# Layer 3's half products grouped by four behind the scores, and the second layer's score matrices made in layer 1's tail

## The chip, the cores and the metric

The kernel runs on one core of a Trainium2 chip. The metric is the device time of one execution in microseconds (us). A core has five engines that run their own instruction streams and wait for each other through semaphores: TensorE (PE in the profile, its weight loads PEld), VectorE (DVE), ScalarE (ACT), GpSimd (POOL) and SyncE (SP), which here only starts transfers (DMAs). Matmuls write into PSUM, which has eight banks per partition; the other data lie in SBUF, 128 partitions wide.

## The reference, cut to what matters

The network has two layers. The first is a residual block of three "approximate matrix multiplications" with normalisations between them; the second is an attention layer and isn't touched. One such multiplication splits its input channels into groups (codebooks), scores each group against 16 centroids, takes a softmax over the 16 and multiplies the softmax by a table:

```python
scores = 2.0 * jnp.einsum('blcs,cks->blck', v, centroids) - jnp.sum(centroids * centroids, -1)[None, None]
attn = jax.nn.softmax(scores * inv_temp, axis=-1)
out = jnp.einsum('blck,cko->blo', attn, lut)
```

This is done three times: 1024 to 256 channels (here "layer 1"), 256 to 256 with 3x3 patches ("layer 2"), 256 to 1024 ("layer 3"), each followed by a batch norm over all images, so that a layer has to end before the next begins. There are 32 images of 14x14, in all 6272 tokens.

## The kernel before, in words

All matmuls are f32. Layers 1 and 2 work through 128 "units" each (`units`, lines 701 to 755): 16 pairs of images times 8 blocks of codebooks. A unit is: scores on TensorE (`score1` at line 879 with 32-row matmuls, `score2` at 999 with 64-row and at 1008 with 32-row ones), exponentials on ScalarE (566), a transpose on VectorE (578), sums, reciprocals and a second transpose on VectorE (597, 599, 605), the normalising product on GpSimd (612), a small repair of table rows by DMA (699), and the table product on TensorE (717, `lut`). The scores of a unit run three or four units ahead of its table product; `side(i)` and `side2(i)` hang other work into step i, and `at(i, piece)` puts a piece into layer 1's step i. Each engine executes what it is given in the order of the program.

A score matmul needs a matrix with the centroids laid out in blocks and a bias. `score_matrices` (341) and `centre` (331) build the matrices on VectorE from raw centroids and masks; `score_biases` (357) squares and centres the centroids on VectorE, and its inner function `biases` multiplies them out on TensorE (388, tile pb) and reduces the result on VectorE (392 to 398). For layer 2 this stands between the layers, at lines 959 to 987: the biases, the matrices w8, five products of an identity (`warm`, 561) and the matrices wm. Ahead of it there are the batch norm of layer 1 (310 to 327), the first padded images (`store_pair`, 909) written to DRAM as h1d, the patches read back from there (`load_patches`, 940), and the tables of layer 2 made ready (`less`, 674 and 675).

Layer 1 reads its pairs of images into three SBUF buffers in turn (pool p1x, `load_x`).

Layer 3 (lines 1066 to 1221) works through 14 chunks of 448 tokens. A chunk has 64 codebooks in 8 groups g of 128 rows; `rows[g]` holds the softmax and `luts[g]` the table. For each of the 8 output blocks m, `product` (1169) accumulates 7 whole products (groups 1 to 7, 128 rows, `whole`) and one half product: group 0 has only 64 rows, which are kept doubled (`double3`, 1116 and 1117) so that output m uses rows 0 to 63 and output m+1 rows 64 to 127, and the two run side by side. The order in a chunk is by pairs of outputs: whole products of m0, half products of m0 and m0+1, whole products of m0+1, then both are copied out (1200) with their statistics (1201). The scores of the next chunk (`score3`, 1093) come in two halves, b = 0 at the head of the chunk and b = 1 behind the first pair; their softmax follows behind outputs 1 and 3. The finished rows are spread by four DMAs and doubled by two (`spread3`, `double3`). A chunk's output is stored to DRAM (o3d, 1218). The first chunk differs: its first three outputs run group by group.

PSUM is divided into four banks for scores (ps_sc), three for outputs (ps_po) and one for small things (ps_tr, tag "tr"). At chunk 3 a transpose for the attention layer's tables (477, tile ph) uses ps_tr, and at chunk 13 the check for overflow does (622, pf).

A second copy of the three layers (`layers(True)`) is in the program for inputs whose exponentials overflow; it isn't executed here.

Of the kernel before, what the change touches and what calls it, by code (L numbers as in the profile page):

```python
# [10 lines left out]
F32 = mybir.dt.float32  # L11
AF = mybir.ActivationFunctionType
ALU = mybir.AluOpType
# [4 lines left out]
P = 128  # L18
# [132 lines left out]
def conv_preact_kernel(ctx: ExitStack, tc: tile.TileContext, a: dict, out: bass.AP):  # L151
# [176 lines left out]

    SHIFT = 32.0

    def centre(pool, i, name, v, k):

        rows, groups = v.shape[:2]
        mean = pool.tile([rows, groups], F32, tag=f"cmean{i}{name}", name=f"cmean{i}{name}")
        t = pool.tile([rows, 1], F32, tag=f"cinvt{i}{name}", name=f"cinvt{i}{name}")
        nc.vector.tensor_scalar(t, invs[i][:rows], k, None, ALU.mult)
        nc.vector.tensor_reduce(mean, v, AX.X, ALU.add)
        nc.vector.tensor_scalar(mean, mean, t, 1.0 / KC, ALU.mult, ALU.mult)
        nc.vector.scalar_tensor_tensor(v, v, t, bc(mean, 2, KC), ALU.mult, ALU.subtract)

    def score_matrices(pool, i, name, raw, mask):


        rows, groups = raw.shape[:2]
        w = pool.tile([rows, groups, P], F32, tag=f"cw{i}{name}", name=f"cw{i}{name}")
        centre(pool, i, name, raw, 2.0)
        for g in range(0, groups, 4):
            m = min(4, groups - g)
            nc.vector.tensor_tensor(
                w[:, g : g + m].rearrange("p g (c k) -> p g c k", k=KC),  # L350
                raw[:, g : g + m].unsqueeze(2).to_broadcast([rows, m, 8, KC]),
                mask.unsqueeze(1).unsqueeze(3).to_broadcast([rows, m, 8, KC]),
                ALU.mult,
            )
        return w

    def score_biases(ps_tr, pool, tmp, i, raw, rows, groups, mask, per, order=None):

# [8 lines left out]
        sq = room[:, : groups * KC].rearrange("p (g k) -> p g k", k=KC)  # L369
        spread = room[:, 512 : 512 + P]  # L370
        cols = sq
        bias = pool.tile([P, n], F32, tag=f"cbias{i}", name=f"cbias{i}")
        nc.vector.tensor_copy(spread.rearrange("p (c k) -> p c k", k=KC), bc(mask, 2, KC))

        nc.vector.tensor_tensor(sq, raw, raw, ALU.mult)
# [10 lines left out]
        def biases():  # L386
            pb = ps_tr.tile([P, 512], F32, tag="tr", name=f"pb{i}")[:, : n * KC]
            nc.tensor.matmul(
                pb, spread, cols.rearrange("p n k -> p (n k)"), start=True, stop=True
            )  # L390
            pv = pb.rearrange("p (n k) -> p n k", k=KC)
            nc.vector.tensor_tensor(pv, pv, bc(kmask, 1, n), ALU.mult)
            b = pool.tile([P, n], F32, tag=f"cb{i}", name=f"cb{i}")
            nc.vector.tensor_reduce(b, pv, AX.X, ALU.add)
            dst, src = bias, b
            if order is not None:
                dst, src = order(bias), order(b, True)
            nc.vector.tensor_scalar(dst, src, -SHIFT, None, ALU.add)
# [92 lines left out]
    def layers(exact, early=None):  # L491
# [142 lines left out]
        two = ExitStack()  # L634
        tsp = two.enter_context(tc.tile_pool(name="p12t", bufs=1))

        def unit_tiles(n):

            ts = []
            for k in range(n):  # L640
                t = tsp.tile([P, 4, NCP], F32, tag=f"t{k}", name=f"t{k}")
                nc.gpsimd.memset(t[:, :, N2:], 1.0)
                ts.append(t)
            return ts
# [114 lines left out]
        stats1 = big.tile([P, 2, NP, 6], F32, tag="stats", name="stats1")  # L759
        with ExitStack() as s:  # L760
            once = s.enter_context(tc.tile_pool(name="p1c", bufs=1))
            xp = s.enter_context(tc.tile_pool(name="p1x", bufs=3))
            sm = s.enter_context(tc.tile_pool(name="p1s", bufs=2))
            st = s.enter_context(tc.tile_pool(name="p1tt", bufs=1 if exact else 2))

# [8 lines left out]

            def load(p):
                def piece():
                    xts[p] = load_x(xp, p)
                    v = slice(2 * p, 2 * p + 2)
                    for k, f in enumerate(
                        gn_pieces(sm, ps_tr, xts[p], gn_a[:, :, v], gn_b[:, :, v])  # L780
                    ):
                        at(first(p) + k, f)

                return piece
# [52 lines left out]
            xts[0] = load_x(xp, 0)  # L837
            for b in range(2):
                luts[b][1]()
            xts[1] = load_x(xp, 1)  # L840
            for b in range(2, 8):
                luts[b][1]()
            if not exact:
# [29 lines left out]
            def score1(u):  # L873
                p, b = divmod(u, 8)
                scs = []
                for j in range(4):
# [2 lines left out]
                    nc.tensor.matmul(sc, w1[r, b, :], xts[p][r, b, :], start=True, stop=True)  # L879
                    scs.append(sc)  # L880
                return scs

            units(
                AHEAD,
# [14 lines left out]
        with ExitStack() as s:  # L899
# [56 lines left out]
            luts2[3][2]()  # L956
            for b in range(4):
                luts2[b][4]()
            bias2, biases = score_biases(
                ps_tr,  # L960
                once,
                st,
                2,
                raw[2],
                72,
                32,
                mask2,
                1,
                lambda t, src=False: t.rearrange("p (h j b) -> p h b j", h=2, j=4)
                if src  # L970
                else t.rearrange("p (h b j) -> p h b j", h=2, b=4),
            )
            w8 = score_matrices(once, 2, "8", raw8, mask64)
            biases()
            warm(5, pads[0][:, :N2])

            centre(once, 2, "1", raw1, 2.0)
            wm = once.tile([P, 2, 4, P], F32, tag="wm", name="wm")
            for h in range(2):
                nc.vector.tensor_tensor(  # L980
                    wm[:, h].rearrange("p b (c k) -> p b c k", k=KC),
                    raw1[:, h].unsqueeze(1).unsqueeze(2).to_broadcast([P, 4, 8, KC]),
                    mask32.rearrange("p (b c) -> p b c", c=8)
                    .unsqueeze(3)
                    .to_broadcast([P, 4, 8, KC]),
                    ALU.mult,
                )

            def score2(u):
                p, b = divmod(u, 8)  # L990
# [75 lines left out]
        with ExitStack() as s:  # L1066
# [76 lines left out]
                less3(7, h, by_act)  # L1143
            relu3(1, 0)
            relu3(1, 1)
            nxt = [score3(1, 0)]
            rows = sum(map(split3, t3), [])
            softmax(st, 0, t3[0], *token_major(st, t3[0]), steps=(1, 1, 2))
            spread3(rows, (1,))
# [3 lines left out]
            softmax(st, 1, t3[1], *token_major(st, t3[1]), steps=(1, 1, 2))  # L1153
            spread3(rows, range(4, 8))
            double3(rows[0])
            for k in range(NCH):
                more = k + 1 < NCH
                if more and k:
                    nxt = [score3(k + 1, 0)]
                elif not more and not exact:  # L1160
                    add_up(2, 2 * NCH)
                    again = overflow(once)
                if early and k > 0:
# [4 lines left out]
                def product(m, g, r=slice(0, P), start=False, stop=False):  # L1168
# [5 lines left out]
                        stop=stop,  # L1174
                    )

                def whole(m):
                    for g in range(1, CT):
                        product(m, g, start=m % 2 == 0 and g == 1, stop=m % 2 == 1 and g == 7)

                for m0 in range(0, CT, 2):
                    for m in range(m0, m0 + 2 + (k + m0 == 0)):
                        if m not in pos:
                            pos[m] = ps_po.tile([P, 512], F32, tag="po", name="po3")[:, :NC]

                    if k + m0 == 0:
                        for g in range(1, CT):
                            for m in range(3):
                                product(m, g, start=g == 1)
                    elif k > 0 or m0 != 2:  # L1190
                        whole(m0)
                    for m in (m0, m0 + 1):
                        r = slice(64 * (m - m0), 64 * (m - m0) + 64)
                        product(
                            m, 0, r, start=m > m0 and k + m0 > 0, stop=m == m0 or k + m0 == 0
                        )
                    if k + m0 > 0:
                        whole(m0 + 1)
                    for m in (m0, m0 + 1):
                        nc.scalar.copy(o[:, m, :], pos[m])  # L1200
                        nc.vector.bn_stats(stats3[:, m, k, :], o[:, m, :])  # L1201
                        if not more:
                            bn_sum(mv3[:, m, :], stats3, m)
                        if more and m == 0:
                            nxt.append(score3(k + 1, 1))
                        if m in (4, 5):
                            relu3(k + 2, m - 4)
                        if more and m in (1, 3):
                            t = nxt[m // 2]
                            softmax(st, 2 * k + 2 + m // 2, t, *token_major(st, t))  # L1210
                            if m == 1:
                                then = split3(t)
                                spread3(then, (1, 2, 3))
                            else:
                                then += split3(t)
                                spread3(then, range(4, 8))
                                double3(then[0])
                nc.sync.dma_start(o3d[:, :, k * NC : (k + 1) * NC], o)
                if more:
                    rows = then  # L1220
            bn_final(once, None, 3, range(CT), sc3, bi3, mv3)
        act.close()
        return again
# [802 lines left out]
```

## Time and profile before

| What | Value |
|---|---|
| time, median of 3 runs (lowest, highest) | 3702.62 us (3702.26, 3704.74) |
| time of the profiled execution | 3700.99 us |
| span of the profiled execution | 3699.2 us |
| mean granted clock of TensorE | 0.994 |
| layer 1's last table product to layer 2's first scores | 836.7 to 856.3 us |
| layer 2's first table product | 880.1 us |
| layer 3's products, first and last | 1860.3 to 2549.5 us |
| stores of layer 3, o3d | 14 of 1792 KB |

Times in the profile count from the span's start. A row of a timeline gives the start, the duration, engine, line, operation, the tiles written and read, the form (partitions x elements) and how many instructions it merges; in brackets stands the idle time of the engine before it and what ended that. A matmul row's duration contains its way through the array, so neighbours overlap; the distance from start to start tells the pace.

### The profile page before, as it was taken

The numbers are of one execution on the slowest core, as the hardware profiler recorded it, in microseconds if no ns is written. First come the engines' busy times: TensorE is split into PE (matmuls) and PEld (weight loads), VectorE is DVE, ScalarE is ACT, GpSimd is POOL, SyncE is SP. The second block draws the span as 40 slices with busy tenths as digits, with TensorE's granted clock in tenths as the row PEclk, the third lists the DMA queues.
The fourth block names the chain that finished last, engine by engine and source line by source line (L and its number), as shares of the span: only waits on it lengthen the run. The fifth ranks groups of instructions, "written<-read, shape, count | busy, mean of one in ns | idle before, by whom it ended". The sixth has DMA issues, their size and how long they took to land. (4 is left out here: it accounts for less than half of the span.)

```text
span 3699.2 us, 49702 instructions
## 1 busy us (share of the span) xinstructions
PE 3626.1 (98%) x16229; PEld 1999.0 (54%) x16229; DVE 2979.5 (81%) x4291; ACT 1717.9 (46%) x3895; POOL 2307.5 (62%) x1398
## 2 busy tenths in 40 slices
PE   8999999999999999999999999998999999999999
PEld 4555555554554445445444444444666666666666
DVE  8999999987888888888753334333799999999996
ACT  5555555543333333333322222213776676676675
POOL 6999999993454445445421111111988888888887
PEclk9999999999999999999999999999999999999999
DMA  3111111115444434444221111103123233233321
GB/s 110 43 46 44 43 37 32 43 33 134 89 92 87 94 75 94 85 95 84 72 51 53 45 45 45 38 33 130 44 79 93 82 87 91 86 84 85 90 75 44
DMA packets 238331, 260.14 MB, mean 70 GB/s; under 512 B 33380, under 2 KB 235692, under 8 KB 238064
## 3 DMA queue, kind: packets, MB, share of 16 engines
q1 hardware_dynamic: 237280, 256.51, 26.2%
q8 instruction: 131, 2.15, 0.3%
q14 instruction: 136, 1.11, 0.1%
q10 hardware_dynamic: 784, 0.37, 0.0%
HBM read 164.04 MB, written 77.09 MB: 65 GB/s over the span
## 5 line engine op out<-in xcount | busy, mean ns | idle before, releaser
L612 POOL TENSOR_TENSOR t<-t,r 128x1664 f32<-128x1664 f32 (+3 forms) x288 | 1008.5, 3502 | 952.0 <-DVE r L605 771.7
L717 PE MATMUL po<-t,lut 128*128 128x392 f32 x3840 | 1332.1, 499 | 2.7 <-DMA t<-spare 2.5
L717 PEld LDWEIGHTS po<-t,lut 128*128 128x128 f32 x3840 | 710.5, 190 | 593.3 <-issue 122.0
L566 ACT ACTIVATE t<-sc,cbias 128x392 f32<-128x392 f32 (+1 forms) x1136 | 580.0, 594 | 946.2 <-issue 476.1
L1536 PE MATMUL mm<-y,lut 128*128 128x392 f32 x2048 | 710.4, 493 | 0.1
L1169 PE MATMUL po<-t,lut 128*128 128x448 f32 (+1 forms) x1792 | 662.1, 551 | 1.6 <-issue 1.6
L578 DVE STREAM_TRANSPOSE tt<-t 128x1664 f32<-128x1664 f32 (+1 forms) x284 | 541.8, 1908 | 105.4 <-ACT t L566 99.7
L605 DVE STREAM_TRANSPOSE r<-rc 128x1664 f32<-128x1664 f32 (+1 forms) x284 | 546.5, 1924 | 20.8 <-DVE rc L599 0.5
L1758 DVE SCALAR_TENSOR_TENSOR pa<-y,lepe_w,pa 128x406 f32<-128x406 f32 x900 | 537.4, 637 | 3.8 <-PE pa L1740 0.3
L1536 PEld LDWEIGHTS mm<-y,lut 128*128 128x128 f32 x2048 | 370.4, 188 | 243.1 <-issue 6.1
L1169 PEld LDWEIGHTS po<-t,lut 128*128 128x128 f32 (+1 forms) x1792 | 308.7, 189 | 352.0 <-issue 351.3
L597 DVE TENSOR_REDUCE sm<-tt 128x104 f32<-128x832 f32 (+2 forms) x284 | 423.2, 1490 | 7.6 <-POOL tt L581 2.0
L1201 DVE BATCH_NORM_STATS2 stats<-o 128x6 f32<-128x448 f32 x112 | 68.9, 617 | 432.0 <-ACT o L1200 432.0
L581 POOL TENSOR_TENSOR tt<-tt 128x832 f32<-128x832 f32 x128 | 248.4, 1941 | 9.3 <-DVE tt L578 9.3
L599 DVE RECIPROCAL rc<-sm 128x104 f32<-128x104 f32 (+1 forms) x284 | 229.4, 808 | 9.8
L1200 ACT COPY o<-po 128x448 f32<-128x448 f32 x112 | 59.2, 530 | 326.4 <-PE po L1169 278.5
L999 PE MATMUL sc<-patch,cw 64*128 64x392 f32 x1024 | 204.0, 514 | 1.4 <-ACT lut L675 1.4
L614 ACT ACTIVATE sm<-sm 128x104 f32<-128x104 f32 (+1 forms) x284 | 84.9, 299 | 215.3 <-DVE rc L599 213.6
L999 PEld LDWEIGHTS sc<-patch,cw 64*128 64x128 f32 x1024 | 87.5, 184 | 109.5 <-issue 62.0
L1721 POOL TENSOR_TENSOR qr<-qr,zb 128x784 f32<-128x784 f32 x64 | 117.8, 1852 | 42.7 <-DMA zb<-zd 35.1
L1389 ACT ACTIVATE w<-x,tb,gn_a 128x196 f32<-128x196 f32 x248 | 128.3, 517 | 33.4 <-DVE x L1403 19.9
L1545 ACT ACTIVATE e<-mm,kbd 128x392 f32<-128x392 f32 x128 | 74.6, 583 | 145.2 <-PE mm L1536 143.7
(191 smaller groups left out, 4103.7 us busy)
## 6 DMA issues: line engine op xcount, KB each, us to landing
patch<-h1d SPq DMA_DIRECT2D x248, 162.8 KB
x<-in_x_dram SPq DMA_DIRECT2D x32, 784.0 KB
o3d<-o SPq DMA_DIRECT2D x14, 1792.0 KB
x<-in_x_dram SPq DMA_DIRECT2D x64, 392.0 KB
out_dram<-x SPq DMA_DIRECT2D x64, 392.0 KB
o<-o3d SPq DMA_DIRECT2D x62, 392.0 KB
h1d<-pad SPq DMA_DIRECT2D x96, 225.0 KB
t<-spare SPq DMA_DIRECT2D x960, 12.2 KB
```

The lines of the kernel that those rows point to most:

```text
L566: nc.scalar.activation(t[:, j, : sc.shape[1]], sc, AF.Identity if exact else AF.Exp, bias=bias[:, j : j + 1],)
L578: nc.vector.transpose(tt, tf)
L581: nc.gpsimd.tensor_tensor(tv[:, :, :8], tv[:, :, :8], tv[:, :, 8:], ALU.add)
L597: nc.vector.tensor_reduce(sm, tv, AX.X, ALU.add)
L599: nc.vector.reciprocal(rc, sm)
L605: nc.vector.transpose(r, bc(rc, 2, KC))
L612: nc.gpsimd.tensor_tensor(tf[:, v], tf[:, v], r[:, v], ALU.mult)
L717: nc.tensor.matmul(po[h], luts[b][:, j, h * P : (h + 1) * P], ts[u % len(ts)][:, j, :N2], start=(b == 0 and j == j0), stop=(b == 7 and j = ...
L999: nc.tensor.matmul(sc, w8[r, 8 * h + 4 * (j // 2) + g], grid(pbuf[n % NPB][r, j // 2, g]), start=True, stop=False,)
L1169: nc.tensor.matmul(pos[m], luts[g][r, m * P : (m + 1) * P], rows[g][r], start=start, stop=stop,)
L1536: nc.tensor.matmul(pv(), w[kt][:, m0 : m0 + P], ywin(p, first + kt), start=(kt == 0), stop=(kt == 3),)
L1758: nc.vector.scalar_tensor_tensor(acc, neighbours(p, c, offset(k)), lw[:, c, k : k + 1], acc, ALU.mult, ALU.add,)
```

## The change

Layer 3: the scores' second half moves from the first to the second half of the chunk, and both halves stand behind the whole products of output 0 or 4. Right behind them run the half products of four outputs, so four accumulators are open: three in ps_po and every fourth output in ps_tr. Then output m0 is copied out, the softmax of the scores follows, and the whole products of the other three outputs run, each with its own copy-out. In the first chunk the fourth output's whole products run ahead of the half products.

Layer 2's matrices: `matrices2` is hung into layer 1's step 125, the bias product into step 127 (there are 128 steps). Its results lie in one SBUF buffer on the other side of the memory, which until then was the third buffer for images; its temporaries lie in a buffer of layer 1. The code between the layers and the five warming products go.

```diff
-            xp = s.enter_context(tc.tile_pool(name="p1x", bufs=3))
+            xp = s.enter_context(tc.tile_pool(name="p1x", bufs=2))
...
-                    xts[p] = load_x(xp, p)
+                    xts[p] = load_x(kept if p % 3 == 1 else xp, p)
...
+            def matrices2():
+                room = kept.tile([P, CT, N2], F32, tag="x", name="room2")
...
+                bias2, biases = score_biases(
...
+                parts[2] = score_matrices(cut, 2, "8", raw8, mask64, w8), wm, bias2
+
+
+                centre(cut, 2, "1", raw1, 2.0)
+                for h in range(2):
+                    nc.vector.tensor_tensor(
+                        wm[:, h].rearrange("p b (c k) -> p b c k", k=KC),
...
+                at(8 * NP - 1, biases)
+
+            at(8 * NP - 3, matrices2)
...
-            bias2, biases = score_biases(
...
-            w8 = score_matrices(once, 2, "8", raw8, mask64)
-            biases()
-            warm(5, pads[0][:, :N2])
-
-            centre(once, 2, "1", raw1, 2.0)
...
+            w8, wm, bias2 = parts[2]
...
-                if more and k:
-                    nxt = [score3(k + 1, 0)]
-                elif not more and not exact:
+                if not more and not exact:
...
                 def whole(m):
                     for g in range(1, CT):
-                        product(m, g, start=m % 2 == 0 and g == 1, stop=m % 2 == 1 and g == 7)
+                        product(m, g, start=m % 4 == 0 and g == 1, stop=m % 4 > 0 and g == 7)
...
+                def halves(m0):
+                    for m in (m0, m0 + 1):
                         if m not in pos:
+                            pool, tag = (ps_tr, "tr") if m % 4 == 3 else (ps_po, "po")
+                            pos[m] = pool.tile([P, 512], F32, tag=tag, name="po3")[:, :NC]
+                        r = slice(64 * (m - m0), 64 * (m - m0) + 64)
+                        first = k + m0 // 4 == 0
+                        product(m, 0, r, start=m % 4 > 0 and not first, stop=m % 4 == 0 or first)
+
+                def out(m):
+                    nc.scalar.copy(o[:, m, :], pos[m])
+                    nc.vector.bn_stats(stats3[:, m, k, :], o[:, m, :])
...
+                def then(b, t):
+
+                    softmax(st, 2 * k + 2 + b, t, *token_major(st, t))
+                    rows3[k + 1] = rows3.get(k + 1, []) + split3(t)
+                    spread3(rows3[k + 1], range(4 * b + (b == 0), 4 * b + 4))
+                    if b:
+                        double3(rows3[k + 1][0])
...
+                for m0 in (0, 4):
+                    pos[m0] = ps_po.tile([P, 512], F32, tag="po", name="po3")[:, :NC]
+                    if k + m0 == 0:
...
+                    else:
                         whole(m0)
...
+                    t = None
+                    if more and (k or m0):
+                        t = score3(k + 1, m0 // 4)
+                    elif more:
+                        t = nxt
+                    halves(m0)
+                    halves(m0 + 2)
+                    out(m0)
+                    if t is not None:
+                        then(m0 // 4, t)
+                    for m in range(m0 + 1, m0 + 4):
+                        if k + m0 > 0:
+                            whole(m)
+                        out(m)
```

## The prediction

> **What bounds the kernel now.** I read the page first, then TensorE's and its weight loads' timeline in layer 3 and layer 2, then every engine's timeline between layers 1 and 2, last the rows in which VectorE waits beside GpSimd. The page's groups:
>
> ```profile
> PE 3626.1 (98%) x16229; PEld 1999.0 (54%) x16229; DVE 2979.5 (81%) x4291; ACT 1717.9 (46%) x3895; POOL 2307.5 (62%) x1398
> L1169 PE MATMUL po<-t,lut 128*128 128x448 f32 (+1 forms) x1792 | 662.1, 551 | 1.6 <-issue 1.6
> ```
>
> TensorE is busy in 98% of the span and idles 1.6 us in all ahead of layer 3's products, which are 662 us of the time. Whatever shortens TensorE's stream there comes off the end; other engines only matter if they become late. TensorE's timeline gives a chunk's length:
>
> ```profile
> 1907.96 1.03 PE L1093 MATMUL sc<-out,cw 32*128 32x448 f32 x8
> ...
> 1956.98 1.03 PE L1093 MATMUL sc<-out,cw 32*128 32x448 f32 x8
> ```
>
> From one chunk's first scores to the next chunk's: 49.02 us, without a stall. Each f32 product is two instructions ("steps"). The weight loads show the step:
>
> ```profile
> 2098.02 0.19 PEld L1169 LDWEIGHTS po<-t,lut 128*128 128x128 f32 x1 [0.19 <-issue]
> 2098.39 0.19 PEld L1169 LDWEIGHTS po<-t,lut 128*128 128x128 f32 x1 [0.19 <-issue]
> 2099.24 0.30 PEld L1169 LDWEIGHTS po<-t,lut 64*128 64x128 f32 x4 [0.65 <-issue]
> 2100.19 0.30 PEld L1169 LDWEIGHTS po<-t,lut 128*128 128x128 f32 x2 [0.65 <-issue]
> 2100.67 0.19 PEld L1169 LDWEIGHTS po<-t,lut 128*128 128x128 f32 x1 [0.19 <-issue]
> ```
>
> Whole products load every 0.375 us, and a load sits one step ahead of its matmul: the load of 2098.39 belongs to the matmul of 2098.77. From there to 2100.67 there are four steps, two of them a pair of half products (64x128; both halves run in one step). They take 1.90 us, not 4 x 0.375 = 1.50. The two changes of shape, into the pair and out of it, cost 0.40 us, 0.20 each. The period says the same: 112 whole steps, 4 x 2 of half pairs and 2 x 2 of scores are 124 x 0.375 = 46.50 us; 2.52 us are left for 12 changes of shape, 0.21 each. I take 0.205.
>
> **Layer 3, the main term.** Now each chunk has six short groups (four half pairs, two of scores), each fenced by whole products: 12 changes. After the change each half of a chunk runs whole, scores, two half pairs, whole: 3 changes, 6 a chunk. No step is added or dropped. Is one pair behind another free, and scores behind halves not? Layer 2 has both kinds of neighbour:
>
> ```profile
> 1404.37 0.96 PEld L999 LDWEIGHTS sc<-patch,cw 64*128 64x128 f32 x8 [0.56 <-ACT pad L909]
> 1405.89 0.31 PEld L1008 LDWEIGHTS sc<-pad,wm 32*128 32x128 f32 x8 [0.56 <-issue]
> 1406.76 0.30 PEld L717 LDWEIGHTS po<-t,lut 128*128 128x128 f32 x2 [0.56 <-issue]
> ```
>
> Four steps of 64-row pairs take 1.52 us, two of 32 rows 0.87; a step is 0.33 us there, so each group is its steps and 0.20 (half a change at either end): pairs behind each other cost nothing extra, going from 64 to 32 rows a full change. The other direction, 32 to 64, is in no row. Bounds: 0 and 0.205 us; nearest is the row just read, so 0.205. "TensorEngine Tiling (Array Packing)", Key Properties, in the Trainium skill says that every change of the tiling mode drains TensorE, which speaks against a free step from scores to halves; by it the term stays as I have it, without it it would be 25 x 0.205 = 5.1 us better.
>
> Count: chunks 1 to 12 lose 6 changes each, 72; chunk 0 (its first scores are made ahead) goes from 8 to 5; chunk 13, without scores, from 8 to 4. 79 x 0.205 = **16.2 us off**.
>
> What must still hide: the second scores move from about 12 to 29 us into the chunk. Their chain to finished rows, from before:
>
> ```profile
> 2069.47 1.03 PE L1093 MATMUL sc<-out,cw 32*128 32x448 f32 x8
> ```
>
> ```profile
> 2081.04 3.99 POOL L612 TENSOR_TENSOR t<-t,r 128x1792 f32<-128x1792 f32 x1 [35.31 <-DVE r L605]
> ```
>
> ```profile
> 2094.78 2.44 SPq L1113 DMA_DIRECT2D t<-t  x4
> 2097.26 0.51 SPq L1116 DMA_DIRECT2D t<-t  x1
> 2098.90 0.51 SPq L1117 DMA_DIRECT2D t<-t  x1
> ```
>
> Scores to the end of GpSimd's product: 2069.47 to 2085.03, 15.6 us (exponentials, one copy-out, VectorE's four passes, the product). The copies that spread and double the rows begin 0.03 us behind the second tile's product and their last packets end by 2101.0, 6.3 us. Together 21.9. New chunk: 46.5 + 6 x 0.205 = 47.7 us; the second scores start at 23.9 + 5.25 + 0.2 = 29.3, so the doubled rows[0] lie ready at 51.2. The next chunk's halves want them at 47.7 + 5.25 + 0.2 + 0.95 = 54.1: 2.9 us to spare. Spread rows 4 (ready 46.3) are wanted at 50.1. On SP's queue the 1.8 MB store of o3d is issued behind these copies, as now. The fourth accumulator: output 3's bank is copied 0.6 us after 23.9 and wanted again past 30; ScalarE's copy of output 1 waits in its queue behind the sum of the softmax until about 16.5, its bank is wanted at 30. VectorE and GpSimd do the same work, idle for most of layer 3. All hidden.
>
> One price: at chunk 3 the attention tables put one transpose on TensorE that waits for VectorE. Now the scores (1 us) run during that wait (TensorE idles 1.48 us ahead of L477); after the change they stand behind it: **+1.0 us**. By "TensorE: Matmul & The Clock Gate", Part 1, an idle window of about 3.4 us halves the clock; the wait grows to 2.5, so by the page nothing more comes; if it did, the row for it is chunk 13's overflow wait, behind which a run of 14 steps takes 7.1 us in place of 5.46, so +1.7 as my bound.
>
> **Second layer's matrices.** Between the layers:
>
> ```profile
> 848.31 2.07 PE L674 MATMUL less<-lut,less_last 128*128 128x512 f32 x2 [5.46 <-ACT lut L675]
> 850.17 1.91 PE L388 MATMUL pb<-croom 72*128 72x512 f32 x2
> 851.88 4.53 PE L561 MATMUL sc<-pad,ident 128*128 128x392 f32 x10
> 856.34 1.59 PE L999 MATMUL sc<-patch,cw 64*128 64x392 f32 x8
> ```
>
> The bias product (1.7) and ten warming matmuls (4.5) leave this place: 6.2 us is the most that the first scores can gain. What they wait on now is VectorE's masks (wm ends at 855.8). That work, 9.9 us (840.25 to 846.41, 853.68 to 855.80, 852.12 to 853.77), goes into a hole in layer 1's tail:
>
> ```profile
> 834.77 0.57 DVE L754 BATCH_NORM_STATS2 stats<-out 128x6 f32<-128x392 f32 x1 [11.28 <-ACT out L727]
> ```
>
> 11.28 us from 823.49. But GpSimd's last normalising product runs in it, 823.62 to 827.33, and two rows show VectorE standing still for such a product:
>
> ```profile
> 1333.52 3.39 DVE L338 TENSOR_SCALAR cmean3b<-cmean3b,cinvt3b 128x2 f32<-128x2 f32 x1
> 2624.11 1.19 DVE L1668 TENSOR_TENSOR kmm<-ks,hmean 128x32 f32<-128x32 f32 x1
> ```
>
> The first usually takes 0.23, the second 0.18; each ended 0.05 us behind a GpSimd product. The moved work has both forms at its head, so it starts at 827.3 and ends at 837.2. The bias product adds 2 x 0.43 = 0.86 us to TensorE ahead of the last unit, so layer 1's last statistics are wanted at 835.6 and come at 837.2: everything up to the patches shifts by 2.5 us. Then: last table product 850.8, scores 852.7, at half clock (0.85 us for a 0.43 step, as in the rows at 850) until 856.3, done 857.0, exponentials 859.1 instead of 860.84: 1.7 gained. The second scores wait for patches, issued until 855.54 now, 858.0 then, landing some 3 us later, and give back 0.3. From there VectorE's 6.5 us per unit, without a gap from 860.87 to 887, carries the lead into layer 2: **1.5 us off**. Bounds: 5.3 off (no wait at GpSimd, full clock, 6.2 - 0.86); 3 worse (patches and half clock without the warm-up eat all). The middle lies nearest to the rows. x's third buffer on the other side is the same rotation: nothing.
>
> **Sum**, against the profiled execution (3700.99; span 3699.2, 1.8 around it): -16.2 + 1.0 - 1.5 = -16.7, 3684.3. The runs' median, 3702.62, lies 1.63 higher: I predict **3686** (3702.62 - 16.7 = 3685.9). A difference under 0.2% (7.4 us) can't be told from none.
>
> **Rivals.** *Scores to halves is free*: 5.1 better, 3681. For: no row has this direction; against: the opposite one costs 0.20. 8%. *The price belongs to each short group, whatever its neighbours*: layer 3 gives nothing, 3702. For: every short group in layer 3 today stands alone; against: layer 2's four steps in a row. 6%. *Rows come late, slower*: the doubled rows[0] become the wait in place of the changes of shape. The place is the halves of each next chunk, it decides from 2.9 us of delay; 4.2 us eat the gain (1.3 us x 13), and a double held behind the 1.8 MB store (8.5 us from 2107.5) would stall 13 x 5.6 = 73 us: 3759. Against: the order on SP's queue, and no chunk stalls in the trace. 4%. The forecast's own case has 80%; 2% is left for mishaps.
>
> **Chances.** Faster by over 0.2%: forecast and first rival, 0.88; within: the second and part of the rest, 0.07; slower 0.05. Range: the forecast's ends are 3686 - 3.8 - 1 and + 4.5 + 1.7 + 0.6 (second term's bounds, clock, 0.20 or 0.21 a change), the first rival's end lies inside: 3680 to 3693.
>
> **What would show it.** Chunk period 47.7 us; four half pairs as loads x8 in one group behind the scores; no idle time ahead of L1169; the moved masks starting at 827, VectorE's first statistics near 837; first scores near 852. Wrong if loads between scores and halves keep 0.375, if TensorE waits for the doubled rows, or if layer 2's first products don't come before 880.

## The result, and the profile after

The changed kernel takes 3693.75 us (median of 13 runs, 3689.95 to 3698.86), the kernel before 3700.96 us (13 runs, 3697.59 to 3704.74). The ratio is 0.998, with a 95% interval of 0.9973 to 0.9988: 7.2 us faster, where 16.7 were forecast. The profiled execution of after took 3698.86 us (span 3696.9), the slowest of its 13 runs, that of before 3700.99.

Layer 3 got shorter at about the forecast pace. From the page of after, the busy time of the engines and layer 3's products (before: 662.1 us):

```profile
PE 3613.6 (98%) x16219; PEld 2004.2 (54%) x16219; DVE 2984.0 (81%) x4291; ACT 1723.5 (47%) x3895; POOL 2307.0 (62%) x1398
...
L1196 PE MATMUL po<-t,lut 128*128 128x448 f32 (+1 forms) x1792 | 649.8, 547 | 1.3 <-DMA t<-t 1.3
```

TensorE's timeline of after, from one pair of scores to the next (start, duration, what; lines stand 44 further down than before in the attention layer, 27 or 28 in layer 3):

```profile
1937.23 1.03 PE L1121 MATMUL sc<-out,cw 32*128 32x448 f32 x8
1938.19 23.02 PE L1196 MATMUL po<-t,lut 64*128 64x448 f32 x64
1961.14 1.03 PE L1121 MATMUL sc<-out,cw 32*128 32x448 f32 x8
```

Half a chunk takes 23.91 us, so a chunk 47.82 where 49.02 were before and 47.7 forecast. The weight loads show the order: scores, the eight instructions of four half products in one run, whole products:

```profile
1936.39 0.19 PEld L1196 LDWEIGHTS po<-t,lut 128*128 128x128 f32 x1 [0.19 <-issue]
1937.23 0.31 PEld L1121 LDWEIGHTS sc<-out,cw 32*128 32x128 f32 x8 [0.65 <-issue]
1938.19 0.30 PEld L1196 LDWEIGHTS po<-t,lut 64*128 64x128 f32 x4 [0.65 <-issue]
1938.68 0.19 PEld L1196 LDWEIGHTS po<-t,lut 64*128 64x128 f32 x2 [0.18 <-issue]
1939.05 0.19 PEld L1196 LDWEIGHTS po<-t,lut 64*128 64x128 f32 x2 [0.18 <-issue]
1939.90 0.30 PEld L1196 LDWEIGHTS po<-t,lut 128*128 128x128 f32 x2 [0.65 <-issue]
```

Scores to halves: 0.96 us for two steps of 0.375, a full change of 0.21. Half a chunk is 62 steps, 23.25 us; 0.66 are left for three changes, 0.22 each. Counted over the whole of layer 3, the rows that the loads use change 161 times in the trace of before and 82 times in that of after: 79 fewer, as forecast.

From its first to its last product, layer 3 takes 677.6 us in place of 689.2, so 11.6 of the forecast 15.2 appear there (the rest is in the point on chunk 3). But only 2.3 us of them reach the end of the span. What gives them back is the attention layer, of which the change touches no line. Counted from its first matmul to the end it took 1139.6 us before and takes 1148.3 after. The row of its costliest VectorE group, first from the page of before, then from that of after:

```profile
L1758 DVE SCALAR_TENSOR_TENSOR pa<-y,lepe_w,pa 128x406 f32<-128x406 f32 x900 | 537.4, 637 | 3.8 <-PE pa L1740 0.3
```

```profile
L1802 DVE SCALAR_TENSOR_TENSOR pa<-y,lepe_w,pa 128x406 f32<-128x406 f32 x900 | 540.4, 636 | 19.5 <-PE pa L1784 17.1
```

The same 900 instructions of the same length, but VectorE now waits 17.1 us for TensorE's products ahead of them. VectorE, GpSimd, TensorE and ScalarE execute the attention layer in another order in the two traces; whether that explains the wait, the first experiment tells.

That order isn't written down in the kernel. The layer's pieces are collected in a `Plan`, whose `write` plays through a list of estimated costs and lets each free engine take its next ready piece. It walks the engines like this:

```python
engines = {p[0] for p in self.pieces}
...
            for e in engines:
```

`engines` is a set of strings such as "PE" and "DVE". The order of a set of strings differs from one process to the next, and VectorE and GpSimd compete in this list for a lock that one of them holds at a time (`locked`, `port`). Played through for all 120 orders of the five, the list gives two schedules only: with GpSimd ahead of VectorE 1163.8 us long by its own estimates, with VectorE ahead 1171.6. GpSimd's instructions of the attention layer stand in before's trace as the first schedule has them, in after's as the second has them; the traces of the next section say the same of all of VectorE's and ScalarE's too (before's order is that of before with GpSimd first, after's that of after with VectorE first, instruction by instruction). So each build of either kernel draws one of two programs, and the two that were compared had drawn differently.

### The profile page after: what moved, and what is told of

Same layout as the page of the kernel before. It is cut to its first block, busy times and chain, and to the rows that moved or that the text cites. A ratio compares the mean times of both kernels' runs of the same rounds, so it can differ in the third digit from the quotient of the medians.

```text
span 3696.9 us, 49649 instructions
## 1 busy us (share of the span) xinstructions
PE 3613.6 (98%) x16219; PEld 2004.2 (54%) x16219; DVE 2984.0 (81%) x4291; ACT 1723.5 (47%) x3895; POOL 2307.0 (62%) x1398
## 5 line engine op out<-in xcount | busy, mean ns | idle before, releaser
L1196 PE MATMUL po<-t,lut 128*128 128x448 f32 (+1 forms) x1792 | 649.8, 547 | 1.3 <-DMA t<-t 1.3
L1802 DVE SCALAR_TENSOR_TENSOR pa<-y,lepe_w,pa 128x406 f32<-128x406 f32 x900 | 540.4, 636 | 19.5 <-PE pa L1784 17.1
L579 ACT ACTIVATE t<-sc,room 128x392 f32<-128x392 f32 x512 | 258.6, 587 | 600.5 <-issue 374.3
L579 ACT ACTIVATE t<-sc,cbias 128x392 f32<-128x392 f32 (+1 forms) x624 | 320.5, 597 | 418.9 <-PE sc L894 154.8
L1196 PEld LDWEIGHTS po<-t,lut 128*128 128x128 f32 (+1 forms) x1792 | 316.6, 190 | 331.3 <-issue 329.8
L1027 PE MATMUL sc<-patch,room 64*128 64x392 f32 x1024 | 207.7, 517 | 2.7 <-DMA patch<-h1d 2.7
L1027 PEld LDWEIGHTS sc<-patch,room 64*128 64x128 f32 x1024 | 88.9, 186 | 114.2 <-issue 67.6
L1546 ACT ACTIVATE y<-x,gb,ga 128x196 f32<-128x196 f32 x256 | 122.5, 541 | 46.6 <-POOL gb L1509 46.6
```

What stands on the lines that cost most here:

```text
L579: nc.scalar.activation(t[:, j, : sc.shape[1]], sc, AF.Identity if exact else AF.Exp, bias=bias[:, j : j + 1],)
L1027: nc.tensor.matmul(sc, w8[r, 8 * h + 4 * (j // 2) + g], grid(pbuf[n % NPB][r, j // 2, g]), start=True, stop=False,)
L1196: nc.tensor.matmul(pos[m], luts[g][r, m * P : (m + 1) * P], rows[g][r], start=start, stop=stop,)
L1802: nc.vector.scalar_tensor_tensor(acc, neighbours(p, c, offset(k)), lw[:, c, k : k + 1], acc, ALU.mult, ALU.add,)
```

## The experiments

**Theory:** the change is worth about what was forecast, and the draw of the attention layer's order takes about 8.5 us of it. **Rival:** the change itself slows the attention layer, say by leaving queues or buffers in another state.

### Both kernels with both orders

One line, in each kernel; the second order has "DVE" and "POOL" exchanged:

```diff
-        engines = {p[0] for p in self.pieces}
+        engines = ["POOL", "PE", "DVE", "ACT", "SP"]
```

(In these expectations the attention parts of 1139.6 and 1148 us are counted from that layer's first matmul, not from layer 3's last product as they say.)

> The kernel before, with one line fixed: the recording layer of the attention layer walks its five engines in a set of strings, whose order is drawn anew in each build; here the list is fixed with GpSimd ahead of VectorE. Of the 120 possible orders the layer's own planner makes only two schedules, 1163.8 us long by its own estimates with GpSimd first and 1171.6 with VectorE first, and the profiled program of before has the first of them, that of after the second. Theory A (the two profiles differ behind layer 3 by the draw, not by the change): as the profile of before, about 3701 us, attention part 1139.6 us from the last product of layer 3 to the end of the span. Theory B (the change slows the attention layer): also about 3701.

> The kernel before with the list fixed the other way, VectorE ahead of GpSimd. Theory A: the attention part grows by 8 to 9 us (7.8 by the planner's estimates, 8.8 between the two profiles), so about 3709.5 us. Theory B (the order is worth nothing, the change itself slows the attention layer): about 3701, as with GpSimd first.

> The changed kernel with GpSimd ahead of VectorE. Theory A: the change's own gain appears, 3693.75 less 8 to 9 us, so about 3685.5 us and a ratio to the first kernel of this set of about 0.996. Theory B: about 3693.8 us, with an attention part of 1148 us.

> The changed kernel with VectorE ahead of GpSimd, the order that the profiled program of after has. Theory A: as measured for the change, about 3694 us, attention part 1148 us. Theory B: about 3694 us too; the set tells the theories apart by the other two kernels.

Measured, with the profiled execution's parts (us):

| | median (runs) | lowest, highest | layer 3, first to last product | attention, first matmul to end |
|---|---|---|---|---|
| before, GpSimd first | 3701.42 (11) | 3697.90, 3703.60 | 689.2 | 1140.1 |
| before, VectorE first | 3709.85 (11) | 3707.67, 3714.33 | 689.2 | 1148.1 |
| after, GpSimd first | 3682.99 (5) | 3682.60, 3685.65 | 675.7 | 1139.0 |
| after, VectorE first | 3692.02 (5) | 3688.06, 3694.75 | 673.0 | 1147.4 |

The attention part follows the order alone, 8.0 and 8.4 us, with either kernel; so does VectorE's wait (in the two kernels of before, 0.3 us with GpSimd first and 16.9 with VectorE first, put down to the same products). From the page of after with GpSimd first, then with VectorE first (the shares of the chain of work that ended last, and the group from above):

```profile
PE 16%; DVE 6%; ACT 6%; POOL 2%; issue 1%; DMA 0%; DVEq 0%; SPq 0%; ACTq 0%; POOLq 0%
...
L1802 DVE SCALAR_TENSOR_TENSOR pa<-y,lepe_w,pa 128x406 f32<-128x406 f32 x900 | 538.8, 640 | 3.6 <-PE pa L1784 0.3
```

```profile
PE 12%; DVE 10%; ACT 4%; POOL 2%; issue 2%; DMA 2%; SPq 0%; DVEq 0%; POOLq 0%; ACTq 0%
...
L1802 DVE SCALAR_TENSOR_TENSOR pa<-y,lepe_w,pa 128x406 f32<-128x406 f32 x900 | 542.1, 640 | 19.3 <-PE pa L1784 17.0
```

The rival falls. With the order held, the change is worth 18.4 us (GpSimd first) and 17.8 (VectorE first), the difference of the medians of five and eleven runs. The kernel before that was run beside this set took 3708.41 us, which fits VectorE first, 3709.85: it seems to have drawn the other order this time. Against it the four ratios are 0.9979 (0.997 to 0.9988), 1.0005 (0.9996 to 1.0014), 0.9932 (0.9919 to 0.9946) and 0.9959 (0.9945 to 0.9972).

### Each part alone, and the price of a change of shape

The parts are the diff of the change cut in two: layer 3's lines, and all the others. In the third kernel the scores are moved away from the halves:

```diff
+                    t = None
+                    if more and (k or m0):
+                        t = score3(k + 1, m0 // 4)
+                    elif more:
+                        t = nxt
...
                         whole(m0)
-                    t = None
-                    if more and (k or m0):
-                        t = score3(k + 1, m0 // 4)
...
                     halves(m0)
```

> Layer 3's new order alone, with layer 2's matrices made where they were before, and the engine list fixed with GpSimd first. The prediction's steps: -16.2 for 79 changes of shape and +1.0 for the wait of the table transpose, so 3701.4 - 15.2 = 3686.2 us. The traces of the fixed pair have layer 3 at 689.2 and 675.7 us: -13.5, so 3687.9. Were the shape changes worth nothing, and the gain made by the matrices, it would stand near 3701.

> The other part alone: layer 2's matrices made in layer 1's tail, layer 3 as before, engine list fixed with GpSimd first. The prediction: -1.5, so 3699.9 us. If the move is worth nothing, because the second scores wait for patches that land when they landed before: 3701.4. If the fixed pair's difference beyond layer 3 belongs to it: 3701.4 - 4.9 = 3696.5.

> The changed kernel (GpSimd first) with each half chunk's scores issued ahead of the first whole output, 14 products before the halves, in place of right in front of them. Every step is kept; 25 half chunks have four changes of shape in place of three. Prediction's reading (each change costs, 32 to 64 rows too): 25 x 0.21 = +5.3 us, about 3688.3. If the price belongs to each short group whatever stands beside it: 0, about 3683. If scores next to halves were free of a change: 25 x 0.42 = +10.5, about 3693.5.

(The three sets of experiments ran on three chips. The kernel before that ran beside each took 3708.41, 3708.99 and 3709.18 us, so a difference of medians across sets is uncertain by about 1 us beyond the spread of the runs, by these three.)

Measured against 3701.42 of the first set: layer 3 alone 3685.30 us (3684.35 to 3688.07, 5 runs), 16.1 off; the matrices alone 3698.71 (3694.13 to 3702.26, 9 runs), 2.7 off, though its runs overlap with those of before; the scores apart 3690.46 (3687.77 to 3691.37, 5 runs), 7.5 more than the changed kernel of the first set. The weight loads with the scores apart:

```profile
2126.18 0.31 PEld L1121 LDWEIGHTS sc<-out,cw 32*128 32x128 f32 x8 [0.65 <-issue]
2127.15 0.30 PEld L1196 LDWEIGHTS po<-t,lut 128*128 128x128 f32 x2 [0.65 <-ACT o L1220]
...
2132.61 0.30 PEld L1196 LDWEIGHTS po<-t,lut 64*128 64x128 f32 x4 [0.65 <-issue]
...
2134.31 0.30 PEld L1196 LDWEIGHTS po<-t,lut 128*128 128x128 f32 x2 [0.65 <-issue]
```

The scores, 14 whole products, the halves and the other 42 come every 24.11 us (2102.08, 2126.19 and 2150.30 in its trace), 0.20 more than next to each other: one more change of shape. The loads count 24 more changes in layer 3, not the 25 expected, because in chunk 0 the moved scores stand right behind the first half products; that is 4.8 us. So the price belongs to the change, not to the group, and scores to halves is a change like any other. The remaining 2.7 us are not in the pace; 1.7 of them are the half clock after chunk 3's wait, which this profile has and that of after with GpSimd first has not. The last 1.0 is within what medians of two sets can differ by: against the third set's 3684.23 for the same changed kernel the whole difference is 6.2.

### Layer 2's patches from two queues

```diff
-            load_patches(0, 1, 3)
+            load_patches(0, 1, 3, engines=(nc.sync, nc.scalar))
```

> The changed kernel (GpSimd first) with the twelve copies that bring the patches of layer 2's second to fourth scores issued by SP and ScalarE in turn, in place of SP alone. If the second scores' wait for these patches is what eats the matrices' gain: the copies are issued in some 3.5 us in place of 7.2, the second scores start 3 us earlier, and so does layer 2's first table product: 3680 us. If the chain behind (exponentials, sums, spread rows) ends last anyway, or ScalarE's queue holds its copies up: 3683 or later, up to 3686.

Measured: 3684.96 us (3682.52 to 3692.41, 5 runs), no gain. The profiled execution is the slowest of the five. In its trace layer 2's first table product starts 38.0 us behind layer 1's last, the shortest of all (40.7 in the changed kernel with GpSimd first), but the second pair of patches is late for it in turn:

```profile
861.46 1.13 PE L1027 MATMUL sc<-patch,room 64*128 64x392 f32 x4 [2.00 <-DMA patch<-h1d]
...
876.34 4.11 PE L732 MATMUL po<-t,lut 128*128 128x392 f32 x12
880.38 1.58 PE L1027 MATMUL sc<-patch,room 64*128 64x392 f32 x6
884.08 1.30 PE L1027 MATMUL sc<-patch,room 64*128 64x392 f32 x2 [2.11 <-DMA patch<-h1d]
...
886.92 7.66 PE L732 MATMUL po<-t,lut 128*128 128x392 f32 x16
```

The wait of 2.1 us moved behind the first table products, and 16 products that take 5.4 us at the end of layer 1 take 7.7 behind it. It isn't this execution alone: from its first to its last table product layer 2 takes 968.7 us here and 963.7 in the other profile with two queues (below), against 959.9 to 962.8 in the twelve with one.

### Two waits in layer 3 hidden

In the changed kernel the attention tables of chunk 3 and the overflow check of chunk 13 stand ahead of the chunk's first whole output. Here first the tables, then both, are issued behind it:

```diff
-                if early and k > 0:
-                    early.pop(0)(ps_tr)
...
                         whole(m0)
+                    if early and k > 0 and m0 == 0:
+                        early.pop(0)(ps_tr)
```

> The changed kernel with GpSimd first in the engine list once more, as the base of this set: 3683.0 us as before, within 2 us.

> The same, with the attention tables of chunks 1 to 3 issued behind the chunk's first whole output in place of ahead of it. If the table transpose of chunk 3 waits for VectorE as the trace shows (2.5 us idle, and in some executions 14 products at half the clock, 1.7 us more), its wait lies beside 5.3 us of products: 2.5 to 4.2 us off the base, about 3680. If the wait only moves behind the output: 0.

> Also the overflow product of the last chunk issued behind that chunk's first whole output. Its wait is 2.0 us, and behind it 14 products took 5.4, 7.1, 8.2 and 8.4 us in different executions: 2 to 5 us more off, about 3676. If VectorE's sums are not ready 5.3 us later: 0 to 2.

> Also layer 2's patches of the second to fourth scores issued by two queues. In the earlier run layer 2's first table product came 2.7 us earlier and layer 2 took that back; if that holds: no better than without, within 2 us. If that profile was an outlier: 2.7 us off.

Measured, five runs each: the base 3684.23 us (3683.83 to 3689.32), the tables late 3678.43 (3677.26 to 3682.21), both 3678.31 (3675.74 to 3681.06), with the patches too 3678.41 (3676.11 to 3680.81). The first step takes 5.8 us off, more than expected (in the profiles 5.6 in layer 3, of which 1.2 stand behind the overflow check, which this step doesn't touch); its trace has the transpose without a wait, and the scores at their full pace behind it:

```profile
1981.43 23.02 PE L1194 MATMUL po<-t,lut 64*128 64x448 f32 x64
2004.29 0.27 PE L490 MATMUL ph<-ident,hp 128*128 128x128 f32 x1
2004.49 1.03 PE L1121 MATMUL sc<-out,cw 32*128 32x448 f32 x8
```

In the profiles layer 3 takes 677.5 (base, the slowest of its five executions), 671.9 and 668.3 us. The second step's 3.6 us don't show in the medians: that profile, again the slowest of its five, is later by 2.4 us at layer 1's first table product and loses 3.0 more between the layers. Whether that is chance was not settled; the last three kernels are not told apart. Against the kernel before beside them (3709.18, again near the time with VectorE first) the three ratios are 0.9921 (0.9908 to 0.9935), 0.9916 (0.9902 to 0.9929) and 0.9919 (0.9906 to 0.9933). All runs of the three lie below all runs of both kernels of this study; the simplest of them is the change, the order fixed with GpSimd first, and the tables late.

## Why the prediction was wrong, point by point

**The step that failed** is the sum, which was made "against the profiled execution" and left everything behind layer 3 as it was. That would have held for the same program; the attention layer's program is drawn anew, and the other draw costs 8.4 us. With it the forecast would have been 3694.4, where 3693.75 was measured; without it, with the order fixed as in before's trace, it was 3686 against 3682.99 and 3684.23. That 3694.4 is met to 0.7 us is partly luck: the 13 runs of before have a median 1.7 us below the 3702.62 that the forecast started from, and with the order held the change gave 18 us, not 16.7. No rival named this, though line 91 was there to be read and decides, by the list's own estimates, over 7.8 us.

**Changes of shape, -16.2, with +1.0 at chunk 3:** right, slightly too large. Layer 3 alone gave -16.1 in the medians, against the 3701.42 of the first set; in its profile, which has the full clock behind chunk 3's wait, layer 3 takes 674.7 us, 14.5 less than before where 15.2 were forecast. A chunk gets shorter by 49.02 - 47.82 = 1.20 us in place of the forecast 6 x 0.205 = 1.23, 0.4 in all, and chunk 3 costs 1.3 in place of 1.0. The rivals fall: scores to halves is not free, and the price is not the group's.

**Chunk 3:** right in its sign, and a little more than its upper bound is needed. TensorE's idle time ahead of the transpose grew from 1.48 to 2.54 us; in the trace of after 14 products behind it take 7.1 us in place of 5.4. From before, then from after:

```profile
2005.99 1.03 PE L1093 MATMUL sc<-out,cw 32*128 32x448 f32 x8
2008.51 0.33 PE L477 MATMUL ph<-ident,hp 128*128 128x128 f32 x1 [1.48 <-DVE hp L475]
```

```profile
2006.31 0.30 PE L490 MATMUL ph<-ident,hp 128*128 128x128 f32 x1 [2.54 <-DVE hp L488]
2006.45 7.18 PE L1196 MATMUL po<-t,lut 128*128 128x448 f32 x14
```

Four of the seven profiles with that wait show the half clock behind it, three not, as here after with VectorE first:

```profile
2000.98 0.30 PE L490 MATMUL ph<-ident,hp 128*128 128x128 f32 x1 [2.54 <-DVE hp L488]
2001.12 5.49 PE L1196 MATMUL po<-t,lut 128*128 128x448 f32 x14
```

I had priced this at up to 1.7 us and left it out, because the Trainium skill, "TensorE: Matmul & The Clock Gate", Part 1, has the clock halve after an idle window of about 3.4 us. Here the half clock came behind a wait of 2.54 us in four of seven; the measurement decides. In the three profiles in which that wait is hidden the half clock isn't there. What tells the four from the three was not found. The stretch from scores to scores that holds the transpose is longer than its neighbours by 1.6 us before (14.46 against 12.84), by 2.9 after at the full clock (26.82 against 23.91) and by 4.6 with the half clock (28.5), so the move costs 1.3 or 3.0 where 1.0, with a bound of 2.7, were forecast. The missing 3.6 us of layer 3 in the profile of after are 2.0 at chunk 3, 1.2 behind the overflow check (14 products in 8.35 us there, 7.13 before), and the 0.4 of the pace. In the profile without either half clock, after with VectorE first, layer 3 is 16.2 us shorter than in before; 1.7 of these come from the overflow check, where before has the half clock, so that like for like it is 14.5 here too.

**Matrices, -1.5:** the size agrees with the profiles, whose ranges overlap; the way there was only in part the forecast's. VectorE stood still behind GpSimd, but not from the start of the moved work; from VectorE's and GpSimd's timelines of after:

```profile
825.01 0.18 DVE L387 COPY croom<-mask 72x128 f32<-72x128 f32 x1
...
826.54 2.85 DVE L349 TENSOR_SCALAR cut<-cut 72x32 f32<-72x32 f32 x1
...
837.39 0.56 DVE L769 BATCH_NORM_STATS2 stats<-out 128x6 f32<-128x392 f32 x1
```

```profile
825.22 4.13 POOL L625 TENSOR_TENSOR t<-t,r 128x1664 f32<-128x1664 f32 x1 [0.30 <-DVE r L618]
```

An instruction of 0.24 us took 2.85 and ended 0.04 us behind GpSimd's product; the four ahead of it had run at their usual lengths, from 825.01 on and partly beside that product, where the forecast had the whole work wait for its end. The statistics followed at 837.39 (forecast 837.2) and the first scores at 852.67 (forecast 852.7). That these times are met is luck: this execution's layer 1 had started 2.2 us later than before's, so counted from there both came over 2 us earlier than forecast. The first scores came 13.8 us behind layer 1's last product in place of 20.0, and the second ones gave most of that back to the patches:

```profile
852.67 2.24 PE L1027 MATMUL sc<-patch,room 64*128 64x392 f32 x8
...
859.44 0.89 PE L1027 MATMUL sc<-patch,room 64*128 64x392 f32 x2 [0.89 <-DMA patch<-h1d]
861.35 1.64 PE L1027 MATMUL sc<-patch,room 64*128 64x392 f32 x2 [1.02 <-DMA patch<-h1d]
863.74 1.64 PE L1027 MATMUL sc<-patch,room 64*128 64x392 f32 x2 [0.75 <-DMA patch<-h1d]
```

From layer 1's last table product to layer 2's first, four profiles without the move took 40.7 to 43.7 us (mean 42.2), eight with it and one patch queue 38.9 to 42.5 (mean 40.5): 1.7 us off. But that count starts behind the moved bias product, which makes layer 1's tail 0.86 us longer, as forecast: from layer 1's 1801st table product, ahead of all moved work, to its last one it is 42.48 us in every profile without the move and 43.34 in every one with it. Counted from that 1801st product, the move is worth 0.8 us to layer 2's first table product (means 84.6 and 83.9) and 1.6 to its last (1046.7 and 1045.1; single profiles 1046.0 to 1047.4 and 1043.7 to 1046.5). Alone the move measured 2.7 in the medians, on top of layer 3's change 1.1 to 2.3. My test for this step, layer 2's first product ahead of 880 us from the span's start, was a bad one: it was 880.9, because layer 1's own start varies from 45.8 to 50.8 us between executions.

**Rows late:** no. In the trace of after every half chunk takes 23.91 us from scores to scores or from halves to halves but for those of chunk 0, whose second takes 24.03, and one each in chunks 3 and 13, so nothing waits for spread or doubled rows; the 1.3 us that the page puts on the DMA stand behind the overflow check at 2488.5, where TensorE idles for 1.6 us before too.

## What to carry to other kernels

Before two programs are compared, see that they differ only where the change is: where a scheduler walks a set of strings, each build may be another program, and here that draw was half as large as the change. Fix such an order, or compare the instruction orders of the two traces layer by layer, before anything is put down to the change. And a wait on an engine that bounds the kernel costs more than its length where the clock falls behind it: look for work of the same engine to set in front of it.

## What the runs showed of the hardware that was not expected

- The half clock came behind less idle time than I had taken: 2.54 us in layer 3. In the trace of after the steps have 0.75 us in place of 0.375 from 2008.28 to 2011.21, some 2 us after work had resumed. The same wait was without it in three of seven profiles. Behind the overflow check, where TensorE idles twice, for 1.8 to 1.9 and 1.3 to 1.6 us around two short products, 14 products take 7.1 to 8.4 us in eleven of the twelve profiles that have these waits, and 5.4 in one. The rows of 2004 to 2014 us in the trace of after, around chunk 3's wait (busy time of PE, PEld, DVE, ACT and POOL with the number of instructions, the granted clock, DMA share, GB/s), show the half clock:

```profile
2004.00:2008.00 4.00, 1.69 (x5) 1.04 (x6) 2.01 (x11) 0.34 (x1) 0.00 (x0) 0.97 0.39 132
2008.00:2011.00 3.00, 3.00 (x5) 1.35 (x4) 0.00 (x0) 0.00 (x0) 0.00 (x0) 0.50 1.05 405
2011.00:2014.00 3.00, 3.00 (x11) 1.26 (x13) 0.00 (x0) 0.00 (x0) 0.00 (x0) 0.98 0.21 77
```

- A change of the rows that a matmul uses (128, 64, 32) cost 0.20 to 0.22 us in every direction seen, and neighbours of one shape cost nothing.
